# Direct transfers of a last tile of 127 rows, each made as two of 112 and 15 rows

## Chip, cores and metric

The kernel runs on one core of one Trainium2 chip. The metric is the device time of one execution in microseconds (us). The changed kernel is compared with the kernel before by that time.

## What is computed

One layer of a graph network over N = 3327 nodes with 1024 features. Cut to what matters:

```
h  = maximum(layernorm(x), 0)                 # x: (3327, 1024) f32
f  = h @ Wf + bf ;  g = h @ Wg + bg           # 1024 x 1024 weights
e  = relu(f @ g.T)
scores    = where(adj > 0, e, -9e15)          # adj: (3327, 3327) int32, about 17 ones in a row
attention = softmax(scores, axis=1)
out = x + attention @ (h @ W + bW)
```

The adjacency matrix is sparse, so few scores of a row count.

## The kernel before

Two paths stand in the program: `edge_path` (line 289) does the work for sparse rows, and `dense_path` (line 31) follows in a branch that is taken only when some row has too many edges. In the profiled execution the branch isn't taken. The change touches `edge_path` alone.

Rows go in tiles of 128 on the 128 partitions. 3327 = 25 x 128 + 127, so there are 26 tiles, numbered 0 to 25, and tile 25 has 127 rows.

**First stage** (lines 357 to 589, about the first 400 us). For each tile `t` the loop at line 535 does three things.

- `degrees(t)`: SyncE (SP) loads 128 rows of `adj` into tile `a` (L431). ScalarE (ACT) turns them into f32 in `r` and counts the degrees (L433). GpSimd (POOL) multiplies `r` by the column numbers (L434). There are two buffers each of `a` and `r`.
- `normed(t)`: SP loads 128 rows of `x` into `xt` (L404, three buffers). VectorE (DVE) takes the row statistics with two BN_STATS and a BN_AGGR for odd tiles, tile 25 among them (L410, L412), or ACT does for even tiles (L418, L421). ACT normalises (L425), and its queue stores the tile to the table `hd` in HBM (L426). A load of `xt` has to wait until the store of the tile that held the buffer three tiles earlier has landed.
- `edges(t, r)`: DVE finds the column numbers of the ones, first 16 MAX over pieces of `r` (L443, tile `cand`), then five rounds of MAX and MATCH_REPLACE (L450, L452) that leave up to 40 numbers in `lst` and `pay`. It marks the degree of each row (L458, `oh`), TensorE (PE) adds these marks up over the tiles in the PSUM tile `pre` with two matmuls (L461, L466), and between the two DVE reads the count (L463, `hit`). So the `hit` of one tile and the two matmuls of the next follow each other in turn.

Between these the weight product A = Wf Wg^T is made on PE (L511), and `make_rows` at line 520 makes two bias rows with 32 small matmuls (L529), whose results DVE splits into three bf16 parts (`split3`, L343 to L354). ACT's queue stores `pay` to the table `pd` in HBM by `store_lists` (L471 for groups of full tiles, L475 for tile 25).

**Sorting** (lines 548 to 584). When the marks of all 26 tiles are in, DVE and PE sort the rows by degree into `perm` (L549 to L583).

**Second stage** (line 592 on, about 400 us to the end). For each of 26 groups of 128 sorted rows POOL gathers, with indirect transfers (L608), the rows of `hd` (`hp`), of `pd` (`pi`) and of `x` (`xp`), and for each neighbour number `k` the rows of `hd` of the neighbours (`G`, 468 gathers). DVE takes a dot product with each (L671) and, after the softmax, adds them up (L711); PE projects. The first gather, of `hp`, needs `perm` and every store to `hd`; the gathers of `pi` need the stores to `pd`, and with the load of `W_sb` (L593) they also wait for the last instruction of `split3` (L354), since their tiles lie on memory of the first stage.

The Tile framework decides in which order the instructions stand on each engine, by a cost model of its own, and each engine runs its own list in that order; a wait at one instruction holds up all behind it. The order is thus part of what a change of the source can change.

Of the kernel before, what the change touches and what calls it, by code (L numbers as in the profile page):

```python
# [8 lines left out]
FP = mybir.dt.float32  # L9
# [279 lines left out]
def edge_path(ctx: ExitStack, tc: tile.TileContext, x, adj, Wf, bf, Wg, bg, W, bW, out, flag):  # L289
# [9 lines left out]
    nc = tc.nc  # L299
    N, D = x.shape  # L300
    O = W.shape[1]
    P = 128
# [7 lines left out]
    def rows(t):  # L310
        return min(P, N - t * P)

    const = ctx.enter_context(tc.tile_pool(name="const", bufs=1))
    wts = ctx.enter_context(tc.tile_pool(name="wts", bufs=1))
    dram = ctx.enter_context(tc.tile_pool(name="dram", bufs=1, space=DRAM))
    hd = dram.tile([N, D], FP, name="hd")
    pd = dram.tile([N, PW], I32, name="pd")
# [39 lines left out]
    with ExitStack() as part1:  # L357
# [30 lines left out]
        pay = c1.tile([P, NT, PW], I32, name="pay")  # L388
# [11 lines left out]
        def normed(t):  # L400

            n = rows(t)
            xt = ln.tile([P, D], FP, name="xt")
            nc.sync.dma_start(xt[:n], x[t * P : t * P + n, :])  # L404
            rstd = ln.tile([P, 1], FP, name="rstd")
            nmr = ln.tile([P, 1], FP, name="nmr")
            if t % 2:
                st = ln.tile([P, D // CB, 6], FP, name="st")
                for c in range(D // CB):
                    nc.vector.bn_stats(st[:n, c, :], xt[:n, c * CB : (c + 1) * CB])  # L410
                mv = ln.tile([P, 2], FP, name="mv")
                nc.vector.bn_aggr(mv[:n], st[:n])  # L412
                nc.scalar.activation(nmr[:n], mv[:n, 0:1], AF.Copy, scale=-1.0)
                nc.scalar.activation(rstd[:n], mv[:n, 1:2], AF.Sqrt, bias=eps[:n])
            else:
                sums = ln.tile([P, 2], FP, name="sums")
                j = lnj.tile([P, D], BF, name="lnj")
                nc.scalar.activation(j[:n], xt[:n], AF.Copy, accum_out=sums[:n, 0:1])  # L418
                nc.scalar.activation(nmr[:n], sums[:n, 0:1], AF.Copy, scale=-1.0 / D)
                j = lnj.tile([P, D], BF, name="lnj")  # L420
                nc.scalar.activation(j[:n], xt[:n], AF.Square, bias=nmr[:n], accum_out=sums[:n, 1:2])  # L421
                nc.scalar.activation(rstd[:n], sums[:n, 1:2], AF.Sqrt, bias=eps[:n], scale=1.0 / D)
            nc.vector.reciprocal(rstd[:n], rstd[:n])
            nc.scalar.activation(nmr[:n], nmr[:n], AF.Copy, scale=rstd[:n])
            nc.scalar.activation(xt[:n], xt[:n], AF.Relu, bias=nmr[:n], scale=rstd[:n])  # L425
            nc.scalar.dma_start(hd[t * P : t * P + n, :], xt[:n])  # L426

        def degrees(t):
            n = rows(t)
            a = apool.tile([P, N], I32, name="a")  # L430
            nc.sync.dma_start(a[:n], adj[t * P : t * P + n, :])  # L431
            r = kpool.tile([P, N], FP, name="r")
            nc.scalar.activation(r[:n], a[:n], AF.Relu, accum_out=deg[:n, t : t + 1])  # L433
            nc.gpsimd.tensor_mul(r[:n], r[:n], iotaj[:n])  # L434
            return r
# [32 lines left out]
        def store_lists(t0, t1):  # L468
            full = min(t1, N // P)
            if full > t0:  # L470
                nc.scalar.dma_start(  # L471
                    pd[t0 * P : full * P, :].rearrange("(t p) k -> p t k", p=P), pay[:, t0:full, :]
                )
            if t1 > full:
                nc.scalar.dma_start(pd[full * P :, :], pay[: rows(full), full, :])  # L475

        def transposed(to, of):

# [56 lines left out]
        for t in range(NT):  # L535
            r = degrees(t)
            normed(t)
            edges(t, r)
            if t % 4 == 3 and t > 4:
                store_lists(t - 7, t - 3)  # L540
            if t < KD:
                load_Wg(t)
            elif t < 2 * KD:
                make_A(t - KD)
        store_lists(20, NT)


# [54 lines left out]
    small = ctx.enter_context(tc.tile_pool(name="small", bufs=3))  # L602
# [155 lines left out]
    for i, (s, k0, k1) in enumerate(units):  # L758
# [7 lines left out]
        if i + 1 < len(units):  # L766
            s2, a, b = units[i + 1]
# [6 lines left out]

    bad = small.tile([P, 1], FP, name="bad")
    nc.vector.tensor_reduce(bad, bads, AX.X, ALU.max)
    onesf = small.tile([P, P], FP, name="onesf")
    nc.vector.memset(onesf, 1.0)
    ps = p_o.tile([P, CB], FP, name="ps_o")
    nc.tensor.matmul(ps[0:1, 0:1], bad, onesf[:, 0:1], start=True, stop=True)  # L780
# [3 lines left out]
def kernel(tc: tile.TileContext, x, adj, Wf, bf, Wg, bg, W, bW, out):  # L784

    nc = tc.nc
    with tc.tile_pool(name="flag", bufs=1) as fpool:
        flag = fpool.tile([1, 1], I32, name="flag")  # L790
        edge_path(tc, x, adj, Wf, bf, Wg, bg, W, bW, out, flag)
        bad = nc.values_load(flag[0:1, 0:1], min_val=0, max_val=1 << 20)
        with tc.If(bad > 0):
            dense_path(tc, x, adj, Wf, bf, Wg, bg, W, bW, out)
# [27 lines left out]
```

## Time and profile before

| what | value |
|---|---|
| median of 3 runs | 1794.35 us (1793.04 to 1795.7) |
| the profiled execution's own time | 1794.12 us |
| its span, first to last instruction | 1792.4 us |
| mean granted TensorE clock | 0.812 of full speed |
| DVE busy | 1478.6 us, 82% of the span |
| PE busy | 1069.6 us, 60% |
| POOL busy | 827.9 us, 46% |
| ACT busy | 296.9 us, 17% |
| bytes moved | 372.37 MB, mean 208 GB/s |

The span is 1.7 us shorter than the execution's own time, which lies within the three runs. Busy times are sums over the whole span, and a wait is shown in a view as idle time of an engine with the event that ended it in brackets behind the instruction (`[69.22 <-DMA xt<-in_x_dram]`: 69.22 us idle, ended by that transfer). A transfer is told by its destination and source (`hd<-xt`); SPq and ACTq are the queues of SP and ACT, and the time of their rows is that of issuing, not of the transfer. In rows of windows stand the busy time of each engine with the number of instructions, then the clock granted to PE, the mean busy share of the core's 16 DMA engines, and GB/s.

### The profile page before, as it was taken

Reading aid. Unit: us, or ns where it says so; the run is one execution under the profiler, and the core shown is the slowest. Engines: PE = TensorE matmul, PEld = TensorE weight load, DVE = VectorE, ACT = ScalarE, POOL = GpSimd, SP = SyncE. Lnnn points to the kernel's source line nnn. Section 1 sums busy time; section 2 is a strip of 40 time slices with the busy share of each in tenths; the row PEclk is TensorE's granted clock in tenths of the full one; section 3 lists DMA queues with packets and bytes.
Section 4 is the critical chain, followed back from the end, with each engine's and each line's share of the span. In section 5 each row is a group of like instructions: output and inputs, shape, how many; then the busy total and the mean of one; then the engine's idle time right before and its main releaser. Section 6 shows DMA issues by size and latency. Waiting matters only on the chain.

```text
span 1792.4 us, 10947 instructions
## 1 busy us (share of the span) xinstructions
PE 1069.6 (60%) x2824; PEld 493.0 (28%) x2824; DVE 1478.6 (82%) x2798; ACT 296.9 (17%) x480; POOL 827.9 (46%) x625
## 2 busy tenths in 40 slices
PE   1278980354007736477364777766686959697833
PEld 1134440021003313133131333323332424233311
DVE  5877860377999899999999999999999899988850
ACT  6666650100001011011000000000000001000100
POOL 7667570115455344553455544444454445435510
PEclk9999995567558868788687888888898979898866
DMA  8888850029678576773676655655665656646320
GB/s 319 306 329 298 292 190 27 28 84 376 210 233 292 168 223 222 236 238 137 222 270 224 242 214 191 226 197 211 212 244 203 232 191 252 205 170 214 100 65 17
DMA packets 124312, 372.37 MB, mean 208 GB/s; under 512 B 40905, under 2 KB 41305, under 8 KB 120913
## 3 DMA queue, kind: packets, MB, share of 16 engines
q0 software_dynamic: 106288, 286.92, 46.8%
q1 hardware_dynamic: 10800, 70.49, 10.7%
q10 hardware_dynamic: 7152, 14.18, 2.1%
q8 instruction: 24, 0.39, 0.1%
q14 instruction: 48, 0.39, 0.1%
HBM read 343.63 MB, written 27.80 MB: 207 GB/s over the span
## 4 chain that ended last, share of the span: by engine, by line
DVE 27%; PE 27%; issue 22%; POOL 9%; DMA 7%; another core or an unknown queue 4%; ACT 2%; POOLq 0%; ACTq 0%; DVEq 0%
DVE y L711 15%; PE ps_o L726 14%; PE q L648 8%; POOL r L434 5%; DVE junk L671 5%; DMA G<-hd,pi 4%; POOL G L608 3%; DVE cand L443 2%; PE ps_A L511 2%; PE ps_t L619 2%; DMA hd<-xt 1%; ACT r L433 1%; DVE sc L671 1%; DVE lst L450 1%
## 5 line engine op out<-in xcount | busy, mean ns | idle before, releaser
L608 POOL DMA_INDIRECT G<-hd,pi x468 | 505.2, 1080 | 418.8 <-DVE y L711 163.3
L671 DVE CUSTOM_DVE_ANT_0 junk<-G,q,ci 128x1024 bf16<-128x1024 f32 (+1 forms) x468 | 597.3, 1276 | 44.6 <-DMA G<-hd,pi 26.4
L711 DVE SCALAR_TENSOR_TENSOR y<-G,sc,y 128x1024 f32<-128x1024 f32 (+1 forms) x442 | 566.2, 1283 | 32.1 <-ACT y L709 23.0
L726 PE MATMUL ps_o<-W_sb,yT 128*128 128x512 f32 (+1 forms) x832 | 402.6, 640 | 1.3 <-ACT yT L620 1.3
L648 PE MATMUL q<-A_sb,hT 128*128 128x512 f32 (+1 forms) x832 | 372.6, 601 | 14.1 <-ACT hT L620 7.5
L619 PE MATMUL ps_t<-ident,y 128*128 128x128 f32 (+1 forms) x208 | 48.1, 408 | 488.6 <-DVE y L711 267.9
L434 POOL TENSOR_TENSOR r<-r,iotaj 128x3327 f32<-128x3327 f32 (+1 forms) x26 | 188.3, 7250 | 131.8 <-ACT r L433 127.4
L726 PEld LDWEIGHTS ps_o<-W_sb,yT 128*128 128x128 f32 (+1 forms) x832 | 166.9, 207 | 207.0 <-issue 198.1
L648 PEld LDWEIGHTS q<-A_sb,hT 128*128 128x128 f32 (+1 forms) x832 | 154.4, 190 | 201.6 <-issue 187.4
L619 PEld LDWEIGHTS ps_t<-ident,y 128*128 128x128 f32 (+1 forms) x208 | 38.7, 214 | 495.6 <-issue 273.1
L443 DVE MAX8 cand<-r 128x8 f32<-128x208 f32 (+2 forms) x416 | 134.0, 360 | 47.9 <-POOL r L434 47.9
L511 PE MATMUL ps_A<-WgT,WfT 128*128 128x512 f32 x256 | 126.3, 655 | 0.5 <-ACT WfT L483 0.5
L620 ACT COPY yT<-ps_t 128x512 f32<-128x512 f32 (+1 forms) x52 | 29.9, 585 | 521.3 <-PE ps_t L619 521.3
L608 POOL DMA_INDIRECT hp<-hd,perm x26 | 27.8, 1068 | 172.0 <-PE ps_t L619 118.7
L433 ACT ACTIVATE r<-a 128x3327 f32<-128x3327 int32 (+1 forms) x26 | 77.1, 2967 | 56.4 <-DMA a<-in_adj_dram 54.7
L608 POOL DMA_INDIRECT xp<-in_x_dram,perm x26 | 34.6, 1329 | 94.7 <-DMA out_dram<-xp,perm 83.1
L410 DVE BATCH_NORM_STATS2 st<-xt 128x6 f32<-128x512 f32 (+1 forms) x26 | 17.7, 680 | 69.2 <-DMA xt<-in_x_dram 69.2
L511 PEld LDWEIGHTS ps_A<-WgT,WfT 128*128 128x128 f32 x256 | 53.0, 211 | 76.6 <-issue 68.4
L687 ACT ACTIVATE sc<-sc,nm 128x11 f32<-128x11 f32 (+11 forms) x32 | 9.8, 308 | 372.6 <-DVE nm L683 272.6
L620 ACT COPY hT<-ps_t 128x512 f32<-128x512 f32 (+1 forms) x52 | 28.0, 588 | 251.4 <-PE ps_t L619 226.8
L736 POOL DMA_INDIRECT out_dram<-xp,perm x26 | 31.8, 1222 | 74.0 <-DVE rs L696 34.0
L466 PE MATMUL pre<-oh,low 128*128 128x64 bf16 x26 | 5.4, 207 | 101.5 <-DVE hit L463 101.5
(131 smaller groups left out, 746.9 us busy)
## 6 DMA issues: line engine op xcount, KB each, us to landing
a<-in_adj_dram SPq DMA_DIRECT2D x25, 1663.5 KB, 9.4
xt<-in_x_dram SPq DMA_DIRECT2D x25, 512.0 KB, 4.3
hd<-xt ACTq DMA_DIRECT2D x25, 512.0 KB, 6.7
G<-hd,pi POOLq DMA_INDIRECT x468, 5.9
wr<-in_L_gnn_Wg_dram SPq DMA_DIRECT2D x8, 512.0 KB, 6.4
wr<-in_L_gnn_Wf_dram SPq DMA_DIRECT2D x8, 512.0 KB, 6.6
W_sb<-in_L_gnn_W_dram SPq DMA_DIRECT2D x1, 4096.0 KB
a<-in_adj_dram SPq DMA_DIRECT2D x1, 1650.5 KB
```

What stands on the lines that cost most here:

```text
L433: nc.scalar.activation(r[:n], a[:n], AF.Relu, accum_out=deg[:n, t : t + 1])
L434: nc.gpsimd.tensor_mul(r[:n], r[:n], iotaj[:n])
L443: nc.vector.max(cand[:n, s * 8 : s * 8 + 8], r[:n, s * SW : min(N, (s + 1) * SW)])
L511: nc.tensor.matmul(ps, WfT[:, k, :], WgT[:, k, o * CB : (o + 1) * CB], start=(k == 0), stop=(k == KD - 1))
L608: nc.gpsimd.indirect_dma_start(out=to, out_offset=None, in_=table, in_offset=bass.IndirectOffsetOnAxis(ap=idx, axis=0),)
L619: nc.tensor.transpose(ps[:, k, :n], of[:n, (g + k) * P : (g + k + 1) * P], ident[:n, :n])
L620: nc.scalar.copy(to[:, g : g + 4, :n], ps[:, :, :n])
L648: nc.tensor.matmul(qo, hT[:, k, :n], A_sb[:, k, o * CB : (o + 1) * CB], start=(k == 0), stop=False)
L671: nc.vector.tensor_tensor_reduce(junk[:n], g[:n], e["q"][:n], 1.0, e["ci"][:n], op0=ALU.mult, op1=ALU.add, accum_out=e["sc"][:n, k : k + 1],)
L711: nc.vector.scalar_tensor_tensor(y, G[s, k][:n], p, y, op0=ALU.mult, op1=ALU.add)
L726: nc.tensor.matmul(ps[:n], yT[:, k, :n], W_sb[:, k, o * CB : (o + 1) * CB], start=(k == 0), stop=False)
L736: ins = nc.gpsimd.indirect_dma_start(out=out[:, :], out_offset=bass.IndirectOffsetOnAxis(ap=perm[:n, s : s + 1], axis=0), in_=e["xp"][:n], ...
```

## The change

A function `pieces(t)` cuts the rows of a tile at the greatest multiple of 16. A tile of 128 rows stays one piece; tile 25 becomes rows 0 to 111 and rows 112 to 126. The four direct transfers of tile 25 in the first stage (loads of `a` and `xt`, stores to `hd` and `pd`) are issued once for each piece. Apart from that the tile `onesf`, of which only the first column is read at the end, shrinks from 128 columns to one.

```
+    def pieces(t):
+        n = rows(t)
+        m = n - n % 16
+        return [(0, m), (m, n - m)] if 0 < m < n else [(0, n)]
...
-            nc.sync.dma_start(xt[:n], x[t * P : t * P + n, :])
+            for a, m in pieces(t):
+                nc.sync.dma_start(xt[a : a + m], x[t * P + a : t * P + a + m, :])
...
-            nc.scalar.dma_start(hd[t * P : t * P + n, :], xt[:n])
+            for a, m in pieces(t):
+                nc.scalar.dma_start(hd[t * P + a : t * P + a + m, :], xt[a : a + m])
...
-            nc.sync.dma_start(a[:n], adj[t * P : t * P + n, :])
+            for b, m in pieces(t):
+                nc.sync.dma_start(a[b : b + m], adj[t * P + b : t * P + b + m, :])
...
-                nc.scalar.dma_start(pd[full * P :, :], pay[: rows(full), full, :])
+                for b, m in pieces(full):
+                    nc.scalar.dma_start(pd[full * P + b : full * P + b + m, :], pay[b : b + m, full, :])
...
-    onesf = small.tile([P, P], FP, name="onesf")
+    onesf = small.tile([P, 1], FP, name="onesf")
```

The framework also orders the last rows of the first stage anew; outside this stretch the lists of all engines stay as they were. Lines of the changed kernel lie 7 to 10 further on (L404 is L411, L410 is L417, L426 is L434, L431 is L440, L433 is L442, L443 is L452, L463 is L472).

On SP, at the end of the first stage, before:

```order
L431 DMA a<-in_adj_dram 128x3327
L431 DMA a<-in_adj_dram 127x3327
L404 DMA xt<-in_x_dram 127x1024
L593 DMA W_sb<-in_L_gnn_W_dram 128x8x1024
L792 TENSOR_LOAD flag
```

On SP at the same place now:

```order
L440 DMA a<-in_adj_dram 128x3327
L440 DMA a<-in_adj_dram 112x3327
L440 DMA a<-in_adj_dram 15x3327
L411 DMA xt<-in_x_dram 112x1024
L411 DMA xt<-in_x_dram 15x1024
L603 DMA W_sb<-in_L_gnn_W_dram 128x8x1024
```

Nothing changed places there; two issues have become four.

On ACT, from the f32 copy of tile 24 to the stores of the lists, before (`lnj` belongs to tile 24, `nmr<-mv 127x1` to tile 25):

```order
L433 ACTIVATE r,deg<-a 128x3327
L514 COPY A_sb<-ps_A 128x512
L426 DMA hd<-xt 128x1024
L419 ACTIVATE nmr<-sums 128x1
L433 ACTIVATE r,deg<-a 127x3327
L421 ACTIVATE lnj,sums<-xt,nmr 128x1024
...
L425 ACTIVATE xt<-xt,nmr,rstd 127x1024
L426 DMA hd<-xt 127x1024
L471 DMA pd<-pay 128x5x41
L475 DMA pd<-pay 127x41
L525 COPY c_sb<-ps_u 128x1
```

The same now:

```order
L442 ACTIVATE r,deg<-a 128x3327
L524 COPY A_sb<-ps_A 128x512
L434 DMA hd<-xt 128x1024
L426 ACTIVATE nmr<-sums 128x1
L428 ACTIVATE lnj,sums<-xt,nmr 128x1024
L442 ACTIVATE r,deg<-a 127x3327
...
L432 ACTIVATE xt<-xt,nmr,rstd 127x1024
L434 DMA hd<-xt 112x1024
L434 DMA hd<-xt 15x1024
L480 DMA pd<-pay 128x5x41
L485 DMA pd<-pay 112x41
L485 DMA pd<-pay 15x41
```

One step of tile 24 (`lnj`) now stands ahead of the f32 copy of tile 25 instead of behind it, and both stores are two.

On DVE, behind the first numbers of tile 23's list (`lst` of 128 rows), before; `cand<-r 128x8` is tile 24:

```order
L450 MAX lst<-cand 128x8
L410 BN_STATS st<-xt 127x6
L452 MATCH_REPLACE cand<-lst,cand 128x128
L410 BN_STATS st<-xt 127x6
L450 MAX lst<-cand 128x8
L443 MAX cand<-r 128x8
...
L443 MAX cand<-r 128x8 x3
L423 RECIPROCAL rstd<-rstd 128x1
```

The same now, up to the second BN_STATS of tile 25:

```order
L459 MAX lst<-cand 128x8
L461 MATCH_REPLACE cand<-lst,cand 128x128
...
L452 MAX cand<-r 128x8 x9
L472 SCALAR_TENSOR_TENSOR hit,rp<-pre,oh 128x64
L430 RECIPROCAL rstd<-rstd 128x1
L452 MAX cand<-r 128x8 x2
L472 SCALAR_TENSOR_TENSOR hit,rp<-pre,oh 128x64
L452 MAX cand<-r 128x8
L417 BN_STATS st<-xt 127x6
L472 SCALAR_TENSOR_TENSOR hit,rp<-pre,oh 128x64
...
L417 BN_STATS st<-xt 127x6
```

The statistics of tile 25 stood ahead of nearly all of tile 24's search; now they stand behind it, among the `hit` of the tiles before.

## Prediction

> **What bounds the kernel now.** I read the page first, then the windows, the waits, the timeline and the chain around 250 to 400 us. In the page, the slices of 45 us show one hole. These rows are the busy share of PE, DVE and POOL in tenths, then GB/s:
>
> ```profile
> PE   1278980354007736477364777766686959697833
> DVE  5877860377999899999999999999999899988850
> POOL 7667570115455344553455544444454445435510
> GB/s 319 306 329 298 292 190 27 28 84 376 210 233 292 168 223 222 236 238 137 222 270 224 242 214 191 226 197 211 212 244 203 232 191 252 205 170 214 100 65 17
> ```
>
> From slice 9 on DVE is the bound. In slices 6 and 7 nothing computes and the transfers run at 27 GB/s, beside about 300 in slices 0 to 4. Windows across the edge of the hole:
>
> ```profile
> 250.00:252.00 2.00, 2.00 (x21) 1.99 (x20) 0.00 (x0) 2.00 (x8) 2.00 (x1) 1.00 0.92 393
> 252.00:254.00 2.00, 1.73 (x7) 0.89 (x6) 0.48 (x2) 0.86 (x2) 2.00 (x2) 1.00 0.06 27
> 270.00:330.00 60.00, 0.00 (x0) 0.00 (x0) 0.00 (x0) 5.01 (x7) 7.85 (x2) 0.52 0.06 26
> ```
>
> In the first the DMA share is 0.92 at 393 GB/s; in the others it is 0.06, one sixteenth. One of the 16 DMA engines works. What it carries stands in the timeline: the load of `a` for tiles 24 and 25 (first and last start 246.2 and 249.2) and of `xt` for tile 25, and who waits; the last three rows give KB each and the median from issue to landing:
>
> ```profile
> L431 SPq DMA_DIRECT2D a<-in_adj_dram x2: 304/316/328, 246.2 to 249.2; - x2
> 268.40 14.06 SPq L404 DMA_DIRECT2D xt<-in_x_dram  x1
> 318.58 2.98 ACT L433 ACTIVATE r<-a 127x3327 f32<-127x3327 int32 x1 [54.65 <-DMA a<-in_adj_dram]
> 321.73 7.19 POOL L434 TENSOR_TENSOR r<-r,iotaj 127x3327 f32<-127x3327 f32 x1 [51.06 <-ACT r L433]
> 338.40 0.69 DVE L410 BATCH_NORM_STATS2 st<-xt 127x6 f32<-127x512 f32 x1 [69.22 <-DMA xt<-in_x_dram]
> a<-in_adj_dram SPq DMA_DIRECT2D x25, 1663.5 KB, 9.4
> a<-in_adj_dram SPq DMA_DIRECT2D x1, 1650.5 KB
> xt<-in_x_dram SPq DMA_DIRECT2D x25, 512.0 KB, 4.3
> hd<-xt ACTq DMA_DIRECT2D x25, 512.0 KB, 6.7
> ```
>
> The last tile of `a` (127 rows, 1650.5 KB) took 318.58 - 249.2 = 69 us, or 24 GB/s; the same tile of 128 rows takes 9.4 us to land. Behind it on the same engine `xt` took 19.8 us more. DVE, whose next instruction needs that `xt`, stood still for 69.22 us. A third transfer of 127 rows, the store to `hd`, ends the stage, in the chain:
>
> ```profile
> 352.78 22.23 DMA hd<-xt
> 375.22 0.82 issue
> 376.04 1.25 POOL hp L608
> ```
>
> The first gather waits for it: 22.23 us against 6.7 for 128 rows.
>
> **The change, part by part.** *Do 112 and 15 rows spread?* All 128-row transfers do (0.92 above), 127 rows don't; no row here shows 112 or 15. I take 112, a multiple of 16 like 128, to spread, and price the 15 rows both ways. The Trainium skill, "DMA: Bandwidth & Descriptors", "Why a DMA increments its semaphore by 16 and not by 1", says that a transfer uses the largest count up to 16 that divides its slowest dimension, so 127 rows take one engine, 112 sixteen and 15 fifteen; the 0.06 agrees for 127, the others are untried here.
>
> *Loads.* The 112 rows of `a` are issued at 249.2 as now, behind tile 24's 128 rows, whose traffic ends by 252; at 393 GB/s their 1.49 MB take 3.8 us, so about 256. The 15 rows are 0.2 MB: 0.5 us if spread, 8.2 us if they crawl on one engine at 24 GB/s, so 257 to 264. When are they needed? ACT and POOL for tile 24, before:
>
> ```profile
> 263.43 7.23 POOL L434 TENSOR_TENSOR r<-r,iotaj 128x3327 f32<-128x3327 f32 x1 [2.76 <-ACT r L433]
> 263.73 0.20 ACT L419 ACTIVATE nmr<-sums 128x1 f32<-128x1 f32 x1
> 321.56 1.13 ACT L421 ACTIVATE lnj<-xt,nmr 128x1024 bf16<-128x1024 f32 x1
> ```
>
> ACT ends `nmr` at 263.9, now does `lnj` (1.3 with its read-out) first, and can start the copy of tile 25 at 265.2; it ends at 268.4. POOL is busy with tile 24 until 270.66 and then with tile 25 until 277.9. So the load is hidden even at 264. `xt` is issued when the store of tile 22 lands (268.4 at the latest, as now) and takes 4.3, or 2.4 more for 15 rows on one engine: 275.1 at the latest. That too is hidden, as follows.
>
> *Where DVE restarts.* Its stall ends no longer with `xt` but with POOL's tile 24 at 270.7; what DVE still has of tile 23 fills the time since 269.18. Then the order gives 4 MAX of `cand` beside tile 23's last steps, 9 more alone, and the first `hit`. The rows before:
>
> ```profile
> 340.07 0.36 DVE L443 MAX8 cand<-r 128x8 f32<-128x208 f32 x1
> 342.85 0.92 DVE L443 MAX8 cand<-r 128x8 f32<-128x208 f32 x3
> 344.02 0.20 DVE L463 SCALAR_TENSOR_TENSOR hit<-pre,oh 128x64 f32<-128x64 f32 x1
> 346.60 0.22 DVE L463 SCALAR_TENSOR_TENSOR hit<-pre,oh 128x64 f32<-128x64 f32 x1 [0.83 <-PE pre L461]
> 348.62 0.22 DVE L463 SCALAR_TENSOR_TENSOR hit<-pre,oh 128x64 f32<-128x64 f32 x1 [0.96 <-PE pre L461]
> 350.64 0.23 DVE L463 SCALAR_TENSOR_TENSOR hit<-pre,oh 128x64 f32<-128x64 f32 x1 [1.05 <-PE pre L461]
> ```
>
> Before, from the first `cand` to the first `hit` were 344.02 - 340.07 = 3.95 us; the new order has one round of MATCH_REPLACE, `lst` and two `cand` fewer ahead (-1.0) and five more `cand` alone (+1.4), so about 4.3, and the first `hit` comes at 275.0. The next ones are paced by PE: 344.02 to 350.64 is 6.62 us for four, and the BN_STATS that now lie between them fit into DVE's waits there (0.83 + 0.96 + 1.05 = 2.8 us beside 1.3). The fifth `hit` comes at 281.6 instead of 350.64: **69.0 us earlier**. `xt`, there by 275.1, is needed by the first BN_STATS at about 276, 1.2 us behind the first `hit`; tile 25's `r`, there at 277.9, by its first `cand` at about 280, behind the fourth. Behind the fifth `hit` the same work is left as before in nearly the same order, so `perm` is 69.0 us earlier as well.
>
> *The stores.* Before:
>
> ```profile
> 352.78 0.48 ACTq L426 DMA_DIRECT2D hd<-xt  x1
> 372.18 0.18 DVE L583 SCALAR_TENSOR_TENSOR perm<-ps_u,tens 128x26 int32<-128x26 f32 x1
> 376.04 1.25 POOL L608 DMA_INDIRECT hp<-hd,perm  x1 [47.12 <-issue]
> 376.05 0.16 ACT L525 COPY c_sb<-ps_u 128x1 f32<-128x1 f32 x1 [23.30 <-PE ps_u L524]
> 380.73 1.28 DVE L658 CUSTOM_DVE_ANT_0 junk<-hp,u_sb,c_sb 128x1024 bf16<-128x1024 f32 x1 [4.40 <-issue]
> 401.30 0.42 DVE L354 CAST bW<-part_acc 3x512 bf16<-3x512 f32 x1
> 401.98 0.95 POOL L608 DMA_INDIRECT pi<-pd,perm  x1 [15.80 <-DVE bW L354]
> 408.43 0.94 POOL L608 DMA_INDIRECT G<-hd,pi  x1 [2.99 <-ACT hT L620]
> ```
>
> `perm` ends at 372.36, the gather waits until 376.04 for the store. After: `perm` at 303.4; the store issued at 352.78 - 69 = 283.8 lands by 6.7 us (plus 2.4 for 15 rows on one engine) later, 293, ten us before. The gather then starts 0.3 us behind `perm` (as `pi` behind `bW`, 401.72 to 401.98): 303.7, which is 72.4 before 376.04. DVE, which stands idle 4.40 us for `hp`, still waits about 1 us (ready at 376.33 - 69 = 307.3, `hp` there at 308.4), so it moves by the full 72.4, and the `split3` steps behind it, to 401.72, with it. The stores to `pd`, issued before `perm` is made, are needed only by the gather of `pi` at 401.98 - 72.4 = 329.6; they cost nothing.
>
> *Added.* Four issues at 0.33 to 0.48 us (as the row of 352.78) on SP and ACT. On SP only the load of `W_sb` stands behind, which waits for `bW` anyway; on ACT the copy of `c_sb`, ahead of which ACT stands idle 23.30 us for PE. The second pieces of `xt` and `pd` each wait for the last user of their semaphore, a load and a store of tile 23, long landed. `onesf`: at most 0.2 us.
>
> *Sum.* 69.0 + 3.4 = 72.4 us off the execution's own 1794.12 (span 1792.4 and 1.7 around it): 1721.7. The median of the runs is 0.2 above: **1722**.
>
> Bounds: at least 67.7 (338.40 to 270.7, if neither the order nor the store gives anything), at most 69.0 + 3.7 + 2.8 = 75.5 (no waits at the `hit`, if PE isn't at the 0.52 of full clock that it has in the hole). With the spread of the runs (about 1.5 either way): 1717 to 1728.
>
> **The rivals.**
> 1. *The stores don't gain*: 112 rows to HBM crawl like 127. Then the store lands at 283.8 + 22.4 = 306.2, the gather starts at 307.0, and only 69.0 are saved: 1725. Against: the 128-row store takes 6.7.
> 2. *Spread over few engines only.* With four, the 112 rows of `a` take 15 us and stay hidden; with two, 31 us, landing at 283, POOL done at 293.5 instead of 277.9, 13 us behind DVE's need of about 280: 1735.
> 3. *No change.* The Trainium skill, "DMA: Bandwidth & Descriptors", "Rules for kernel authors", advises against two transfers to disjoint partition halves, since both spread over the same engines and serialize. As a mechanism here: the two pieces together take as long as the one, 69 us again, and the time stays 1794. The row of 0.06 speaks against it: fifteen engines stand free.
> 4. *Slower.* It decides if the 112 rows stay on one engine too. Then all waits remain, and `xt` and `hd`, which end the two waits of DVE and POOL, each pay for a second transfer: 0.33 to issue and up to 2.7 until it lands (the shortest landing in the first stage, row below), together 0.7 to 6 us: 1795 to 1800, say 1799. Nothing but the number 127 in the rows speaks for it.
>
> ```profile
> DMA to landing us min/median/max: 2.7/5.3/10.3
> ```
>
> **How the numbers follow.** 0.87 for the forecast, 0.05 for rival 1, 0.02 for rival 2, 0.03 for rival 3, 0.03 for rival 4. The range takes the bounds of the first two, which hold 0.92, and 1 us either way for a second stage whose 468 gathers may fall otherwise: 1716 to 1729. A measurement of this kernel tells 0.2% (3.6 us) from no change. Faster: 0.87 + 0.05 + 0.02 = 0.94; same: rival 3, 0.03; slower: rival 4, 0.03.
>
> **What would show it.** In the changed profile: no window around 250 to 300 us at 27 GB/s and 0.06; `r<-a 127x3327` at about 265 and POOL's tile 25 at 270.7, with no idle between; first `hit` behind `cand` near 275, fifth near 282; the hole of DVE 1.5 us wide; `hd<-xt` landing near 290; first `hp` near 304, its wait ended by `perm`. Wrong would be: DVE still waiting for `xt` or POOL's tile 25 behind 280; the gather of `hp` released by a store; or a second stage (from the first `G`, at 408 before, to the end) that is not as long as it was, 1384 us.

## The result and the profile after

The changed kernel takes 1723.89 us (median of 4 runs, 1722.38 to 1726.45), the kernel before in the same comparison 1793.98 (4 runs, 1793.04 to 1795.7). The ratio is 0.961, with a 95% interval of 0.9593 to 0.9626: 70 us less. The profiled execution took 1724.37 us, its span is 1722.6 us.

The page's slices of the changed kernel (43 us each now), DVE's busy tenths and GB/s:

```profile
DVE  5877868699998999999999999999999898988750
GB/s 322 319 315 292 315 237 74 184 338 198 262 263 170 223 231 231 229 151 256 258 207 181 215 215 256 245 227 211 216 226 198 228 179 257 198 113 227 105 57 17
```

The two slices of DVE at 0 are gone; one at 74 GB/s is left, in which DVE is busy for 38.4 of the 43.1 us, 89%. The timeline of the changed kernel at the places that the prediction named, in order of time: ACT's copy and POOL's product for tile 25, the first `hit`, the first BN_STATS of tile 25, the fifth `hit`, `perm` and the first gather of `hp`.

```profile
268.10 1.47 DVE L452 MAX8 cand<-r 128x8 f32<-128x208 f32 x5
269.65 2.98 ACT L442 ACTIVATE r<-a 127x3327 f32<-127x3327 int32 x1 [2.56 <-issue]
272.60 0.38 DVE L452 MAX8 cand<-r 128x8 f32<-128x208 f32 x1
272.80 7.21 POOL L443 TENSOR_TENSOR r<-r,iotaj 127x3327 f32<-127x3327 f32 x1 [0.23 <-ACT r L442]
276.88 0.20 DVE L472 SCALAR_TENSOR_TENSOR hit<-pre,oh 128x64 f32<-128x64 f32 x1
278.05 0.67 DVE L417 BATCH_NORM_STATS2 st<-xt 127x6 f32<-127x512 f32 x1
282.44 0.23 DVE L472 SCALAR_TENSOR_TENSOR hit<-pre,oh 128x64 f32<-128x64 f32 x1
304.10 0.18 DVE L593 SCALAR_TENSOR_TENSOR perm<-ps_u,tens 128x26 int32<-128x26 f32 x1
304.58 1.08 POOL L618 DMA_INDIRECT hp<-hd,perm  x1 [24.58 <-DVE perm L593]
337.48 0.94 POOL L618 DMA_INDIRECT G<-hd,pi  x1 [2.95 <-issue]
```

Of the idle times of 50 to 70 us around the hole none is left. The BN_STATS has no wait behind it, so `xt` was there in time, and the gather of `hp` waits for `perm` and no longer for the store. The transfers of tile 25, from the DMA issues of the changed kernel (the last number is the time from issue to landing in us):

```profile
a<-in_adj_dram SPq DMA_DIRECT2D x1, 1455.6 KB, 10.9
xt<-in_x_dram SPq DMA_DIRECT2D x1, 448.0 KB, 3.6
hd<-xt ACTq DMA_DIRECT2D x1, 448.0 KB, 3.1
a<-in_adj_dram SPq DMA_DIRECT2D x1, 194.9 KB, 11.6
xt<-in_x_dram SPq DMA_DIRECT2D x1, 60.0 KB, 3.4
hd<-xt ACTq DMA_DIRECT2D x1, 60.0 KB, 2.9
```

Where one transfer took 69 us, its two pieces land 11 to 12 us after their issue; the store's pieces take 3 us instead of 22.

### The profile page after: what moved, and what is told of

Its sections match the earlier page's. It is cut to its first block, busy times and chain, and to the rows that moved or that the text cites. A ratio compares the mean times of both kernels' runs of the same rounds, so it can differ in the third digit from the quotient of the medians.

```text
span 1722.6 us, 10956 instructions
## 1 busy us (share of the span) xinstructions
PE 1072.5 (62%) x2824; PEld 494.5 (29%) x2824; DVE 1477.0 (86%) x2798; ACT 297.0 (17%) x480; POOL 823.7 (48%) x625
## 4 chain that ended last, share of the span: by engine, by line
issue 23%; DVE 22%; PE 20%; DMA 10%; POOL 4%; ACT 1%; POOLq 0%; DVEq 0%; ACTq 0%
DVE y L721 15%; PE ps_o L736 12%; DMA G<-hd,pi 6%; PE q L658 5%; DVE junk L681 5%; POOL G L618 3%; DMA out_dram<-xp,perm 2%; PE ps_t L629 2%; DVE sc L681 1%; DMA pi<-pd,perm 1%; DMA xp<-in_x_dram,perm 1%; PE ps_o L737 1%; DVE xp L745 0%; POOL out_dram L746 0%; DMA hp<-hd,perm 0%
## 5 line engine op out<-in xcount | busy, mean ns | idle before, releaser
L443 POOL TENSOR_TENSOR r<-r,iotaj 128x3327 f32<-128x3327 f32 (+1 forms) x26 | 188.2, 7249 | 83.0 <-ACT r L442 78.7
L452 DVE MAX8 cand<-r 128x8 f32<-128x208 f32 (+2 forms) x416 | 133.6, 361 | 48.2 <-POOL r L443 48.2
L442 ACT ACTIVATE r<-a 128x3327 f32<-128x3327 int32 (+1 forms) x26 | 77.1, 2966 | 3.6 <-issue 2.6
L745 DVE TENSOR_TENSOR xp<-ps_o,xp 128x512 f32<-128x512 f32 (+1 forms) x52 | 35.8, 688 | 30.1 <-PE ps_o L737 29.9
L618 POOL DMA_INDIRECT pi<-pd,perm x26 | 31.1, 1194 | 47.1 <-issue 19.6
## 6 DMA issues: line engine op xcount, KB each, us to landing
a<-in_adj_dram SPq DMA_DIRECT2D x1, 1455.6 KB, 10.9
```

What stands on the lines that cost most here:

```text
L452: nc.vector.max(cand[:n, s * 8 : s * 8 + 8], r[:n, s * SW : min(N, (s + 1) * SW)])
L618: nc.gpsimd.indirect_dma_start(out=to, out_offset=None, in_=table, in_offset=bass.IndirectOffsetOnAxis(ap=idx, axis=0),)
L745: nc.vector.tensor_add(xo, e["o"][o][:n], xo)
```

## The experiments

The theory: a direct transfer from SP's or ACT's queue runs on as many DMA engines as the largest count up to 16 that divides its rows, so 127 rows, a prime number, run on one; the gain is the hole behind that engine. The rivals: the cut itself or the new order of instructions brings the gain, whatever the sizes; or only multiples of 16 spread; or the stall is that of one transfer alone. All kernels compute the whole layer. Each time stands beside runs of the kernel before on the same chip.

### Other places to cut: 113, 126 and 122 rows

In `pieces`, instead of the multiple of 16:

```
-        m = n - n % 16
-        return [(0, m), (m, n - m)] if 0 < m < n else [(0, n)]
+        return [(0, 113), (113, n - 113)] if n < P else [(0, n)]
```

and the same with 126 and with 122. The order of the instructions on every engine is that of the changed kernel, so only the sizes of the pieces differ.

Cut at 113, expected:

> Tile 25 cut at 113 and 14 rows instead of 112 and 15: as many transfers and the same order of instructions as in the changed kernel, but 113 is prime. Theory (a direct transfer runs on as many DMA engines as the largest count up to 16 that divides its rows): 113 rows stay on one engine; the load of a takes 69 x 113/127 = 62 us and lands near 314, xt 17.6 us behind it near 331, DVE stands at the BN_STATS of tile 25 from 278 to 331, so about 53 us over the changed kernel: 1777, with a DMA share of 0.06 in the hole. Rival (any cut of the 127 rows, or the new order of instructions, does it): 1724.

Measured: 1776.76 us (before 1793.25; ratio 0.9898, 0.9876 to 0.9921). A window inside its hole (start and end, length, busy time of PE, its weight load, DVE, ACT and POOL, the granted clock, the DMA share and GB/s):

```profile
285.00:310.00 25.00, 0.00 (x0) 0.00 (x0) 0.00 (x0) 0.00 (x0) 0.00 (x0) 0.50 0.07 28
```

And in its timeline, where DVE is released, where `perm` is made and where the first gather starts:

```profile
331.74 0.69 DVE L416 BATCH_NORM_STATS2 st<-xt 127x6 f32<-127x512 f32 x1 [14.20 <-DMA xt<-in_x_dram]
357.23 0.18 DVE L592 SCALAR_TENSOR_TENSOR perm<-ps_u,tens 128x26 int32<-128x26 f32 x1
358.44 1.08 POOL L617 DMA_INDIRECT hp<-hd,perm  x1 [35.45 <-DMA pd<-pay]
```

The hole at 28 GB/s is back with two pieces and the new order, and `xt` lands at 331.7 where 331 was expected. So neither the cut as such nor the order brings the 70 us: this kernel is 16.5 us faster than before. At the first gather it is 17.6 us ahead (358.44 against 376.04), and the rows tell where. `xt` landed 6.7 us earlier (331.74 against 338.40). From there to the end of `perm` it takes 25.7 us instead of 34.0, since in the new order DVE has the search of tile 24 behind it before it waits. The gather then waits 1.0 us behind `perm` instead of 3.7. The order is thus worth about 8 us where the hole stays; it isn't what takes the hole away.

Cut at 126, expected:

> Tile 25 cut at 126 and 1 rows. Theory (largest divisor up to 16): 126 rows run on 14 engines, the single row on one (13 KB, under 1 us); everything stays hidden as with 112: 1724. Rival (only multiples of 16 rows spread): 126 rows crawl on one engine, a lands near 321 and xt near 341: about 63 us over the changed kernel, 1787.

Measured: 1721.63 us (ratio 0.9599, 0.9578 to 0.9619), as fast as the changed kernel. 126 is no multiple of 16, so it needn't be one. How many engines it kept busy the time doesn't tell, as long as the load stays hidden.

Cut at 122, expected:

> Tile 25 cut at 122 and 5 rows; 122 = 2 x 61. Theory (largest divisor up to 16): two engines, DMA share 0.12; a takes 33 us and lands near 286, xt 9.5 us behind it near 296 where 278 was needed: 18 us over the changed kernel, 1742. Rival (not divisible by 16: one engine): about 1783. Rival (any even number of rows spreads): 1724.

Measured: 1743.21 us (ratio 0.9719, 0.9698 to 0.974). A window inside its hole:

```profile
270.00:285.00 15.00, 2.07 (x4) 0.30 (x4) 5.46 (x25) 0.00 (x0) 1.08 (x1) 0.58 0.13 55
```

And DVE's release in its timeline:

```profile
297.98 0.69 DVE L416 BATCH_NORM_STATS2 st<-xt 127x6 f32<-127x512 f32 x1 [4.88 <-DMA xt<-in_x_dram]
```

The DMA share is 0.13, two sixteenths, at 55 GB/s, twice the rate of one engine. For 113, 122 and 126 rows the times are 1777, 1743 and 1722, each within 3 us of what the divisor gave. The Trainium skill, "DMA: Bandwidth & Descriptors", "Why a DMA increments its semaphore by 16 and not by 1", states this rule; these runs agree with it for 113 and 122 rows by the share, and for 126 by the time.

### The parts alone

Each of the four transfers was left whole or cut as in the changed kernel. The load of `xt` alone cut:

```
-            nc.sync.dma_start(xt[:n], x[t * P : t * P + n, :])
+            for a, m in pieces(t):
+                nc.sync.dma_start(xt[a : a + m], x[t * P + a : t * P + a + m, :])
```

> Only the load of xt of tile 25 is cut at 112 and 15; a and both stores stay whole. Theory: a keeps one engine busy until about 320, and the share of xt on that engine queues behind it; POOL's tile 25 ends near 331 where 280 was, and the store to hd takes 22 us: 50 to 55 us over the changed kernel, 1773 to 1779. Rival (the stall is that of xt alone, since DVE waited for nothing else): 1727.

Measured: 1773.25 us (ratio 0.9878, 0.9859 to 0.9898). The pieces of `xt` in this kernel, and what waited for `a` and for `xt`:

```profile
xt<-in_x_dram SPq DMA_DIRECT2D x1, 448.0 KB, 52.3
xt<-in_x_dram SPq DMA_DIRECT2D x1, 60.0 KB, 38.4
320.22 2.98 ACT L442 ACTIVATE r<-a 127x3327 f32<-127x3327 int32 x1 [55.77 <-DMA a<-in_adj_dram]
321.39 0.69 DVE L417 BATCH_NORM_STATS2 st<-xt 127x6 f32<-127x512 f32 x1 [50.57 <-DMA xt<-in_x_dram]
```

They needed 52 and 38 us where 3.6 and 3.4 do: `xt` comes 1.2 us behind `a`, so its share on the busy engine queued behind `a`. The stall isn't that of `xt` alone, though DVE waits for `xt`. This kernel is still 20.0 us faster than before, most of it because `xt` comes 17.0 us earlier (321.39 against 338.40): whole, it had needed 19.8 us behind `a` on the one engine.

The other three were timed in one comparison with the changed kernel run again:

> The changed kernel once more, for the comparisons of this call: 1724, 70 us under the kernel before.

It took 1723.48 us (before 1794.31; ratio 0.9602, 0.9589 to 0.9615).

Only the load of `a` cut (the lines of L440 as in the change, the others as before):

```
-            nc.sync.dma_start(a[:n], adj[t * P : t * P + n, :])
+            for b, m in pieces(t):
+                nc.sync.dma_start(a[b : b + m], adj[t * P + b : t * P + b + m, :])
```

> Only the load of a of tile 25 is cut; xt and the stores stay whole. Theory: xt takes 20 us on one engine that is now free, from 264.3 to 284.5, where DVE needs it at 278: 6.5 us; the store to hd then ends near 313.5, 3 us after perm: 9.6 us over the changed kernel, 1733. Rival (xt is as long as a, or waits behind something else): 1750 or more.

Measured: 1733.73 us (ratio 0.9661, 0.9648 to 0.9674). DVE's wait for the whole `xt`:

```profile
286.58 0.69 DVE L417 BATCH_NORM_STATS2 st<-xt 127x6 f32<-127x512 f32 x1 [9.41 <-DMA xt<-in_x_dram]
```

So cutting `a` alone gains 60.6 of the 70.8 us, and `xt` costs about 7 by itself, if the store is the 3 that follow. The parts don't add up: cutting `xt` is worth 20 us while `a` is whole and about 7 once `a` is cut, since the two stand one behind the other on the same engine. The orders differ too: in the kernels with `a` cut DVE has the new order, while with `xt` or the stores alone cut the first BN_STATS of tile 25 stands ahead of tile 24's search, as in the kernel before.

Only the two loads cut, the stores whole:

> Only the loads of a and xt of tile 25 are cut; the stores to hd and pd stay whole. Theory: the store to hd takes 22 us on one engine, from 284.6 to 307, and the first gather of hp starts at 307.8 instead of 304.6: 3.2 us over the changed kernel, 1727. Rival (the store's cover is long enough, it gives nothing): 1724.

Only the stores cut, the loads whole:

> Only the stores of tile 25 are cut; the loads stay whole, and the order of instructions is that of the kernel before. Theory: the hole of 69 us stays, the first gather of hp is released by perm instead of by the store, 3.4 us earlier: 1790.6. Rival (the store to hd isn't the wait that ends last): 1794.

The edits are the first and third pieces of the diff, and the second and fourth. Measured: 1725.3 us (ratio 0.9625, 0.9609 to 0.9641) and 1792.75 us (ratio 0.9993, 0.9984 to 1.0002). By the time alone neither is settled: 1.8 us over the changed kernel and 1.6 under the kernel before, both inside the intervals. The profile settles it. `perm` and the first gather with the loads alone cut:

```profile
303.07 0.19 DVE L593 SCALAR_TENSOR_TENSOR perm<-ps_u,tens 128x26 int32<-128x26 f32 x1
306.98 1.20 POOL L618 DMA_INDIRECT hp<-hd,perm  x1 [28.03 <-DMA pd<-pay]
```

and with the stores alone cut:

```profile
374.25 0.18 DVE L593 SCALAR_TENSOR_TENSOR perm<-ps_u,tens 128x26 int32<-128x26 f32 x1
374.73 1.08 POOL L618 DMA_INDIRECT hp<-hd,perm  x1 [43.70 <-DVE perm L593]
```

With the store whole the gather starts 3.7 us behind the end of `perm`, with the store cut 0.3 us, whatever the loads do: the store is worth 3.4 us at this place. The releaser shown in the first row, `pd<-pay`, is another store on the same queue behind that of `hd`; by the program the gather of `hp` needs only the stores to `hd`. Both stores were cut together here. The next kernel separates them.

### The queue, the tile of ones, and full tiles

The kernel before, with the two loads and the store to `hd` of tile 25 whole, issued on POOL's queue:

```
-            nc.sync.dma_start(a[:n], adj[t * P : t * P + n, :])
+            (nc.sync if n == P else nc.gpsimd).dma_start(a[:n], adj[t * P : t * P + n, :])
```

and so for `xt` and `hd`.

> The kernel before with no cut, but the loads of a and xt and the store to hd of tile 25 (127 rows whole) are issued on POOL's queue instead of SP's and ACT's. Theory A (one engine for 127 rows belongs to the queues of SP and ACT; POOL's queue spreads them): the hole is gone, 1724 to 1732, the upper end if POOL issues late between its multiplications. Rival B (127 rows go to one engine from every queue): about 1794.

Measured: 1725.36 us (before 1794.91; ratio 0.961, 0.9594 to 0.9626). The load of `a` among its DMA issues:

```profile
a<-in_adj_dram POOLq DMA_DIRECT2D x1, 1650.5 KB, 11.8
```

And the window in which it ran:

```profile
264.00:270.00 6.00, 6.00 (x29) 3.48 (x27) 6.00 (x35) 1.19 (x4) 5.30 (x1) 1.00 1.06 228
```

127 rows in one transfer take 11.8 us from POOL's queue, and the DMA share says that all engines work. So it is not the 127 rows alone that make the transfer slow, but 127 rows on the queue of SP or ACT. The Trainium skill, "DMA: Bandwidth & Descriptors", "Why a DMA increments its semaphore by 16 and not by 1", names this exception, and the trace agrees. DVE's BN_STATS of tile 25 stand ahead of the search of tile 24 here, as in the kernel before: the hole goes without a cut and without the new order. POOL issued `a` 11 us later than SP does in the changed kernel (261.9 against 251.1), since it stood behind POOL's products, and the first gather came at 309.6 instead of 304.6, which the time hardly shows. What released this gather:

```profile
309.14 0.18 DVE L583 SCALAR_TENSOR_TENSOR perm<-ps_u,tens 128x26 int32<-128x26 f32 x1
309.61 1.05 POOL L608 DMA_INDIRECT hp<-hd,perm  x1 [19.04 <-DVE perm L583]
```

Of the stores only the one to `hd` was moved, those to `pd` are as before, and the gather starts 0.3 us behind `perm`. It was the slow store to `hd` that held it, or what stood behind that store on ACT's queue.

The changed kernel with `onesf` at 128 columns:

```
-    onesf = small.tile([P, 1], FP, name="onesf")
+    onesf = small.tile([P, P], FP, name="onesf")
```

> The changed kernel with onesf at 128 columns again. Theory: 0.1 us on DVE, nothing to be measured: 1724. Rival (the smaller tile moves other tiles or waits): another time by several us.

Measured: 1722.47 us (ratio 0.9601, 0.9585 to 0.9617): nothing, as expected.

Two kernels cut the full tiles as well, to see what a cut costs where it isn't needed:

```
-        return [(0, m), (m, n - m)] if 0 < m < n else [(0, n)]
+        return [(0, 112), (112, n - 112)]
```

> The loads of a and xt and the stores to hd of all 26 tiles are cut at row 112, into 112 + 16 rows (tile 25 112 + 15), though 128 rows need no cut; the order of instructions in the first stage moves with it. Theory A (a transfer of 112 rows keeps all 16 engines busy but moves 256 GB/s where 128 rows move 396, as seen around 254 to 260 in the changed kernel): the first 250 us, whose DMA share is 0.8 to 0.9, become bound by the transfers: 70 MB at 256 and 8 MB at 396 GB/s are 294 us, so 40 to 50 us over the changed kernel, 1765 to 1775. Rival B (the low rate came from that one place): two more issues of 0.33 us on SP and one on ACT for each tile, hidden: 1724 to 1730.

and at row 64:

> The same with full tiles cut into 64 + 64 rows (4 rows for each of 16 engines) and tile 25 into 112 + 15; the order of instructions in the first stage moves with it. Theory A (any transfer that isn't the whole 128 rows moves less): 1765 to 1775, as with 112. Rival B (it is 112 that is slow, by the rows that fall to each engine): 1724 to 1732.

Measured: 1838.96 us (before 1794.59; ratio 1.0239, 1.0219 to 1.0259) and 1838.82 us (ratio 1.024, 1.0211 to 1.027), 115 us over the changed kernel. That is more than twice what theory A gave, and rival B is out by far. The same window in the changed kernel, in the one cut at 112 and in the one cut at 64:

```profile
50.00:100.00 50.00, 11.87 (x45) 7.94 (x44) 38.72 (x196) 37.07 (x53) 36.08 (x5) 1.00 0.84 302
```

```profile
50.00:100.00 50.00, 9.45 (x40) 6.74 (x40) 29.60 (x128) 22.67 (x32) 23.61 (x4) 1.00 0.81 215
```

```profile
50.00:100.00 50.00, 7.19 (x30) 5.06 (x31) 29.69 (x127) 23.88 (x31) 21.62 (x3) 1.00 0.88 220
```

The engines are as busy as with whole tiles (0.81 and 0.88 against 0.84) and move 215 to 220 GB/s instead of 302. With its tiles cut a kernel moves its bytes more slowly in this window, with 112 + 16 as with 64 + 64. The first gathers of `hp`, cut at 112 and at 64:

```profile
416.05 1.08 POOL L618 DMA_INDIRECT hp<-hd,perm  x1 [17.61 <-DVE perm L593]
417.81 1.08 POOL L618 DMA_INDIRECT hp<-hd,perm  x1 [17.61 <-DVE perm L593]
```

They come 111 and 113 us behind that of the changed kernel (304.58), so nearly all of the loss lies in the first stage. Not all of it is shown to be the rate: the order of instructions there also moved, and SP waited 234 and 204 us in all for stores to `hd` before its loads of `xt`, against 164 in the changed kernel.

## Why the prediction was right

**Spreading.** 112 rows were taken to spread, and they did; the 15 rows, priced both ways, landed 11.6 us after their issue where the 112 of `a` needed 10.9. With that the hole, and nearly all of the gain, was settled.

**The loads** were hidden as forecast, but not by the working. The 112 rows of `a` were to land at about 256, the 15 rows at 257 to 264, and they landed at about 262 and 263: issued at 251.1 in this execution, 10.9 and 11.6 us. The 393 GB/s of the 128-row tile, by which the prediction priced the 112 rows, did not hold for them. Windows of the changed kernel, with the end of tile 24's 128 rows and with tile 25's pieces:

```profile
250.00:254.00 4.00, 4.00 (x30) 3.18 (x28) 0.68 (x5) 3.73 (x10) 4.00 (x1) 1.00 0.97 396
254.00:260.00 6.00, 5.72 (x15) 2.59 (x15) 4.59 (x19) 2.64 (x6) 6.00 (x2) 1.00 1.06 256
```

ACT's copy of tile 25 was to start at 265.2 and started at 269.65. It writes a buffer of `r` (there are two) that DVE still reads for tile 23, until 268.10 + 1.47 = 269.57; the profile names no releaser, but ACT starts 0.08 us behind that end. The prediction looked at the load and at ACT's own queue and left this wait out. POOL then waited 0.23 us for it, so the omission cost next to nothing, but that is luck: the margin that the text claimed (265 to 270) wasn't there.

**The restart** was to be at 270.7, the first `hit` at 275.0 and the fifth at 281.6; they came at 272.60, 276.88 and 282.44. The 1.9 us are already there at SP's issue of the loads of `a` (248.06 against 246.2), ahead of anything that the change moves, and in the second execution of the same kernel that issue came at 245.2: scatter between executions. From restart to fifth `hit` the forecast had 10.9 us, the profile has 9.8. The first `hit` is 4.3 us behind the restart, as forecast; the four that follow take 5.6 us instead of 6.6. The prediction took their pace from rows at half of PE's clock. PE's pairs of small matmuls between them, in the changed kernel:

```profile
277.33 1.87 PE L539 MATMUL ps_A<-WgT,bf 128*3 128x512 f32 x2
281.21 1.02 PE L539 MATMUL ps_A<-WgT,bf 128*3 128x512 f32 x2
```

The granted clock is 0.50 up to 280 us and 1.00 from 281 on; in the kernel before it was still 0.50 up to 350, just short of the fifth `hit` at 350.64. The prediction named this in its bounds and left it out of its sum.

**`perm` and the store.** `perm` was expected to end at 303.4 and ended at 304.28, the gather at 303.7 and started at 304.58, the forecast 0.3 us behind it. Up to the first gather 376.04 - 304.58 = 71.5 us are saved of the forecast 72.4. The store's 3.4 us are confirmed by the two kernels with the parts alone.

**The second stage** was to stay as long as it was, 1384 us from the first `G`; it is 1722.6 - 337.48 = 1385. Over the executions of kernels whose second stage is the same it lies between 1379 (cut at 126) and 1389 (the changed kernel run again), and this scatter is larger than any term of the sum but the hole. That the forecast of 1722 came within 2 us of the median is therefore partly luck: the late start, the faster `hit` and the second stage went different ways.

**The rivals.** The first (stores don't gain) fell by the 3.1 and 2.9 us of the pieces. The second (few engines) has now been run, with 122 rows at a share of two engines: 1743 instead of the 1735 that the prediction gave for 112, since it counted only POOL's delay by `a` and left out `xt`, which runs on the same two engines behind it. The third and fourth fell with the hole; the Trainium skill's advice ("DMA: Bandwidth & Descriptors", "Rules for kernel authors") against two transfers to disjoint partition halves doesn't hold for 127 rows on SP's and ACT's queues, and looks too mild for 128: the kernels with all tiles cut were 2.4% slower than the kernel before.

## What to carry to other kernels

A DMA share of one sixteenth at about 27 GB/s over tens of us was one engine at work here: look for a transfer from SP's or ACT's queue whose number of rows has no large divisor, and cut only that one, since the kernels with full tiles cut were slower; here issuing it whole from POOL's queue did as well. A tail tile's slow transfer also delays what stands behind it on the same queue, so the wait that the profile names (here `xt`) needn't be the transfer that costs (here `a`: cutting it alone gained 60 of the 70 us). When a stall is taken away, list what the next instruction waits for in full, its output buffer too.

## What the runs showed of the hardware that wasn't expected

Transfers that ran on all engines, but not of 128 rows from SP or ACT, kept the engines as busy and moved less: 256 GB/s at a share of 1.06 for 112 and 15 rows, 228 at 1.06 for 127 rows from POOL, against 396 at 0.97 for 128 rows; and from 50 to 100 us 215 and 220 at 0.81 and 0.88 with all tiles cut at 112 and 64, against 302 at 0.84 with whole ones. Which part of a transfer makes it so, the rows that fall to each engine or something else, was not tried.

Behind a transfer that runs on one engine the engine that issues was held up too. In the kernel cut at 113 these issues of SP took 28 and 32 us, where the changed kernel needs 4 and 1:

```profile
245.72 28.14 SPq L439 DMA_DIRECT2D a<-in_adj_dram  x3
273.96 32.22 SPq L410 DMA_DIRECT2D xt<-in_x_dram  x2
```
